# Block products of a sparse attention layer: one 128-column product for a chunk that both halves of a block list, in place of two 64-column products side by side

## The chip, the cores and the metric

The kernel runs on one core of one Trainium2 chip. The metric is the device time of one execution in microseconds (us). A TensorE instruction multiplies a stationary operand (the weights, loaded by a LDWEIGHTS instruction, up to 128 columns) by a moving operand (here 512 columns wide) and adds into a bank of PSUM. A float32 product of this kernel is two such pairs of LDWEIGHTS and MATMUL in the trace. An operand of 64 columns fills half of the array's columns, and its result lies in 64 of a bank's 128 partitions.

## The reference, cut to what matters

`x` is 4096 x 512, `adj` is 4096 x 4096 with about 1% of its entries above zero (weights from 0.05 to 1 at those places, the diagonal always set, the pattern symmetric).

```
# layer 0
h = relu(layernorm(x));  x = x + relu(normalized(adj) @ h @ W + b)
# layer 1
inp = relu(layernorm(x));  h = inp @ W
e = leaky_relu(h @ a[:F] + (h @ a[F:]).T, 0.2);  mask = adj > 0
att =  softmax(where(mask,  e, -1e12), axis=1)
neg = -softmax(where(mask, -e, -1e12), axis=1)
x = x + elu(concat([att @ inp, neg @ inp], axis=1) @ wtrans)
```

The change is in layer 1, in the two products `att @ inp` and `neg @ inp`.

## The kernel before

Layer 0 (to about 960 us) is a dense product with all of `adj`. While it runs, the kernel also makes, from `adj` and for layer 1, lists of the rows that each group of rows needs.

Layer 1 is sparse. The 4096 output rows are cut into 64 blocks of 64 rows, two blocks a pair (`2n` and `2n + 1`). A block is again two halves of 32 rows. The rows of `inp` that a pair needs, with their scores and their mask bytes, are gathered from a table in DRAM into three tiles of SBUF, in chunks of 128 rows: tile 0 with 8 chunks, tile 1 with 7 (6 gathered and, as the last, the pair's own rows), tile 2 with 7 (`LISTED`, `CHUNKS`, lines 43 and 44). The even block of a pair reads tiles 0 and 1, which are its chunks 0 to 14; the odd block reads tiles 1 and 2, its chunks 0 to 13, of which 0 to 6 are tile 1. Tile 1 is so shared by both blocks.

Not every chunk holds rows for both halves of a block. `HALVES` (line 49) lists for the even and the odd block which chunks each half reads:

```python
HALVES = (
    ((0, 1, 2, 3, 4, 10, 11, 12, 13, 14), (3, 4, 5, 6, 7, 8, 9, 10, 11, 14)),
    ((0, 1, 2, 3, 4, 6, 9, 10, 11, 12, 13), tuple(range(11))),
)
```

`weights(r)` (line 1754) makes the attention weights `p` of a block for all its chunks with ScalarE and VectorE: 128 gathered rows by, for each half `h` and each sign `g` of the score, 32 output rows. In `p[:, k]` the four groups of 32 columns lie side by side, so a half is 64 columns (its 32 rows for both signs) and a chunk 128. VectorE then sums `p` over its chunks (line 1787).

`product(r)` (line 1799) is one block's work on TensorE: the sums of the weights (`inverse_sums`, cs, L580), and `half_products` (line 551), the function that is changed. It goes through the two halves' lists side by side: step by step one chunk of half 0 and one chunk of half 1, each a product with 64 weight columns and the 512 columns of the gathered rows, the first into partitions 0 to 63 of the bank `u`, the second into 64 to 127. An even block has 10 such steps, an odd one 11, so a pair has 42 products. In the trace they are `u<-g,p` at L556. ScalarE then scales `u` by the inverse sums into `us` (L1815), TensorE transposes it (tp, L595), and `project1` and `finish1` multiply by `wtrans` (o, L1826). Two more chunks come last for the early pair and the first pair of the loop, from the tile `late_h`, where both halves read both chunks (lines 1574 and 1812).

The order of the loop is written out (line 1903). For block `k` of the order: `product(order[k])`; then gathers for the pair after next (after an even block tile 0, after an odd one tiles 1 and 2); then `weights(order[k + 2])`; then the transposes of block `k - 1`; then half of the projection of an earlier pair. The gathers are indirect DMAs issued by POOL (GpSimd), one for each chunk (L506), and kept in program order. The own rows come through a DMA that SP issues (L520), after the six gathers of tile 1. The tiles are doubled over pairs (`k % 2` in `gather1`, line 1739), and are taken again as whole tiles (`reuse_waits="tile"`): the gathers for the pair after next into a tile wait until the last product that reads the tile has ended. Two early blocks (`product0`, L1567, tile name `p_pair`) are multiplied at the end of layer 0, in the order of the program where `pin` is set. The block products of the loop are not pinned.

Of the kernel before, what the change touches and what calls it, by code (L numbers as in the profile page):

```python
# [32 lines left out]
RB = 64  # L33
# [10 lines left out]
CHUNKS = (8, 7, 7)  # L44
# [4 lines left out]
# [4 lines that stand above are left out]
# [221 lines left out]
def gcn_gat_kernel(  # L274
# [26 lines left out]
    nc = tc.nc  # L301
# [36 lines left out]
    with sbuf(name="init", bufs=1) as init:  # L338
        column = init.tile([P, P], F32, name="column")
        nc.vector.memset(column[:, 0:1], 0.0)  # L340
        n = 1
# [60 lines left out]
    steps = [(c, r) for c in range(NK) for r in range(CAPS[c] // 8)]  # L402
# [148 lines left out]
    def half_products(r, u, p, row, chunks, end=True, pin=False, begin=True):  # L551


        for ks in zip(*chunks):
            for h, k in enumerate(ks):
                i = nc.tensor.matmul(  # L556
                    u[h * RB : (h + 1) * RB],
                    p[:, k, h].rearrange("p g i -> p (g i)"),
                    row(k),
                    start=begin and k == HALVES[r % 2][h][0],  # L560
                    stop=end and k == chunks[h][-1],
                )
                if pin:
                    tc.keep_in_program_order(i)

# [41 lines left out]
    with sbuf(name="y0", bufs=1) as y_pool, sbuf(name="wa", bufs=1) as wa_pool, sbuf(name="bits", bufs=4) as bits_pool, sbuf(name="small0", bufs=4) as small, ExitStack() as rest, ExitStack() as lists:  # L607
# [5 lines left out]
        def list_tables(pool):  # L613
            rank = pool.tile([P, EN], F32, name="rank")
            nc.gpsimd.iota(
                rank,
                [[-1, EN]],
                base=EN,
                channel_multiplier=0,
                allow_small_or_imprecise_dtypes=True,  # L620
            )
            before = pool.tile([P, NE + 1, NH], F32, name="before")
            start = pool.tile([NH, 1], F32, name="start")
            nc.gpsimd.iota(
                start,
                [[0, 1]],
                base=0,
                channel_multiplier=STR,
                allow_small_or_imprecise_dtypes=True,
            )  # L630
            return rank, before, start

        rank, before, start = list_tables(list_pool)
# [400 lines left out]
        def new_rows(pool, n):  # L1034
            rows = [pool.tile([P, ROW_W], F32, tag=f"h{k}", name=f"h{k}", bufs=1) for k in range(n)]
            for h in rows:
                nc.gpsimd.memset(h[:, ROW_T + 1 :], 0.0)
            return rows
# [94 lines left out]
        i0, n = GROUPS[0]  # L1133
# [362 lines left out]
        def early_pair(work, at_pool, prod, rows):  # L1496
# [63 lines left out]
            def product0(r):  # L1560
                u0[r] = bank(f"u{r}")

                def row(k):
                    gt, k0, n = parts0(r)[k >= parts0(r)[1][1]]
                    return gt[:, k - k0, :F].bitcast(F32)

                half_products(r, u0[r], ps0[r], row, HALVES[r % 2], False, r == blocks[0])  # L1567

            def late_product0(r):
                def row(k):  # L1570
                    return late_h[:, k - slots0(r), :F]

                late = range(slots0(r), slots0(r) + n_late)
                half_products(r, u0[r], ps0[r], row, (late, late), begin=False)
                sum0(r, late)
# [77 lines left out]
        with sbuf(name="work0", bufs=2) as work, sbuf(name="rows0", bufs=1) as row_pool, sbuf(name="sums", bufs=3) as sum_pool, sbuf(name="at", bufs=6) as at_pool:  # L1653
# [4 lines left out]
            with tc.manual_schedule(engines=order - {engine.PE}):  # L1658
                rows = new_rows(row_pool, 3)
# [31 lines left out]
    def sparse_layer1():  # L1691
        nonlocal verdict
        with ExitStack() as pools:
# [105 lines left out]
            def product(r):  # L1799
                p, total = wgt.pop(r)  # L1800

                rl = None if r in first else inverse_sums(small, r, total)
                u = bank(f"u{r}")

                def row(k):
                    gt, k0, n = parts(r)[k >= parts(r)[1][1]]
                    return gt[:, k - k0, :F].bitcast(F32)

                half_products(r, u, p, row, HALVES[r % 2], r not in with_late)
                if r in with_late:  # L1810
                    ks = range(n_late)
                    half_products(r, u, lates.pop(r), lambda k: late_h[:, k, :F], (ks, ks), begin=False)
                rl = rl or inverse_sums(small, r, total)
                us[r] = work.tile([P, F], F32, tag="us", name=f"us{r}")
                nc.scalar.activation(us[r], u, AF.Copy, scale=rl)  # L1815
# [169 lines left out]
```

## Time and profile before

| | |
|---|---|
| median of 4 runs | 2025.3 us (2012.46 to 2028.84) |
| the profiled execution | 2015.94 us |
| its span, first to last instruction | 2014.1 us |
| mean granted TensorE clock | 0.98 |
| layer 0, to about 960 us | TensorE busy 947.81 of 960.00 us |
| layer 1 loop, 1100 to 1950 us | TensorE busy 773.01, VectorE 452.38, ScalarE 490.74, POOL 538.19 of 850.00 us |
| end, 1950 to 2014 us, no gathers left | TensorE busy 56.22 of 64.00 us |

In the profile PE is TensorE's matmuls, PEld its weight loads, which overlap with the matmuls, DVE is VectorE, ACT ScalarE, POOL GpSimd and SP the queue of SyncE. A group's line has, in order: line of code, engine, operation, names out<-in, the weights' shape (partitions*columns), the tiles' shapes, the count; then busy time in us and the mean ns of one; then the idle time of the engine just before these instructions and what ended most of it. `g` are the gathered tiles, `p` the attention weights. In the view in order of time, a line is: start, duration, engine, line, operation, names, count, and in brackets the idle time before it with what ended it; instructions that overlap or follow one another closely are merged into one line with their count. In the view of waits a line is: who waited, for what, us in total, how often, the longest. "issue" is idle time for which the profile shows no releaser; "remote" is one that it can't place.

### The profile page before, as it was taken

What the parts mean: (1) busy time and instruction counts of PE and PEld (TensorE: products, weight loads), DVE (VectorE), ACT (ScalarE), POOL (GpSimd) and SP (SyncE); (2) the same over time, 40 slices, a digit from 0 to 9 for tenths busy, and PEclk for the clock granted to TensorE, in tenths of its full rate; (3) what the DMA queues carried; (4) which work ended last, traced back from release to release, by engine and by line L of the source; (5) the groups of instructions that cost most, each with busy time, mean ns of one, the idle gap of its engine ahead of it and who ended that gap; (6) DMA issues with size and microseconds to landing.
All of it is one profiled execution on the core that took longest, in us unless ns stands there. A gap on an engine that the chain in (4) does not pass through costs nothing.

```text
span 2014.1 us, 24509 instructions
## 1 busy us (share of the span) xinstructions
PE 1890.3 (94%) x7708; PEld 1052.6 (52%) x7708; DVE 1272.7 (63%) x2758; ACT 937.3 (47%) x2165; POOL 822.3 (41%) x919
## 2 busy tenths in 40 slices
PE   8999999999999999999679989999899898898988
PEld 3444468888888888884333333333333333333333
DVE  6766588898889979762535655545555465454552
ACT  6777743222223222221436655556565565564551
POOL 3110000024322233305536666566666666666640
PEclk9999999999999999999879999899999999999999
DMA  9999967576858586758857878788888787887860
GB/s 370 396 334 335 321 198 245 175 244 211 265 163 274 171 256 194 243 179 303 266 202 249 278 239 301 235 293 260 282 271 292 241 260 243 265 250 241 259 190 23
DMA packets 217218, 504.33 MB, mean 250 GB/s; under 512 B 35059, under 2 KB 69395, under 8 KB 217078
## 3 DMA queue, kind: packets, MB, share of 16 engines
q0 software_dynamic: 62560, 233.71, 36.3%
q1 hardware_dynamic: 114240, 236.49, 35.1%
q10 hardware_dynamic: 40278, 32.47, 5.2%
q8 instruction: 63, 1.03, 0.2%
q14 instruction: 77, 0.63, 0.1%
HBM read 457.77 MB, written 103.45 MB: 279 GB/s over the span
## 4 chain that ended last, share of the span: by engine, by line
PE 89%; issue 6%; DMA 2%; POOL 2%; DVE 1%; another core or an unknown queue 0%; ACT 0%; ACTq 0%; POOLq 0%; DVEq 0%; SPq 0%
PE p L1105 31%; PE u L556 30%; PE o L1826 10%; PE acc L1064 5%; PE yp L890 5%; PE q L1465 3%; PE tp L595 2%; DMA ar<-in_adj 2%; POOL g L506 2%; PE counts L867 1%; PE cs L1541 1%; PE tx L831 1%; PE o L1860 0%; PE cs L580 0%; DVE key L429 0%
## 5 line engine op out<-in xcount | busy, mean ns | idle before, releaser
L506 POOL DMA_INDIRECT g<-table,idx x672 | 639.5, 952 | 436.0 <-issue 176.4
L556 PE MATMUL u<-g,p 128*64 128x512 f32 x2604 | 622.5, 603 | 87.3 <-issue 75.7
L556 PEld LDWEIGHTS u<-g,p 128*64 128x64 f32 x2604 | 189.3, 138 | 462.6 <-issue 440.1
L442 POOL DMA_INDIRECT ld<-lst,off x160 | 143.7, 898 | 343.2 <-DMA ld<-lst,off 152.1
L1765 ACT ACTIVATE z<-s,g 128x64 f32<-128x64 f32 x812 | 259.6, 320 | 47.1 <-issue 13.3
L1105 PE MATMUL p<-y,at 128*128 128x256 f32 x832 | 248.0, 380 | 0.0
L1105 PE MATMUL p<-y,sums 128*128 128x256 f32 x832 | 247.4, 379 | 0.0
L1105 PE MATMUL p<-t,sums 128*128 128x256 f32 x832 | 245.3, 379 | 0.0
L1826 PE MATMUL o<-wt,ut 128*128 128x512 f32 x496 | 227.0, 601 | 2.1 <-DVE eo L1843 1.4
L1768 DVE TENSOR_TENSOR z<-z,y 128x512 f32<-128x512 f32 (+1 forms) x124 | 80.3, 647 | 204.8 <-ACT y L1767 116.2
L1787 DVE TENSOR_REDUCE total<-p 128x128 f32<-128x1920 f32 (+1 forms) x62 | 207.7, 3350 | 2.1
L1105 PEld LDWEIGHTS p<-t,sums 128*128 128x128 f32 x832 | 158.0, 190 | 21.7 <-issue 0.2
L1105 PEld LDWEIGHTS p<-y,sums 128*128 128x128 f32 x832 | 158.0, 190 | 21.5
L1105 PEld LDWEIGHTS p<-y,at 128*128 128x128 f32 x832 | 157.1, 190 | 23.2 <-issue 2.3
L1826 PEld LDWEIGHTS o<-wt,ut 128*128 128x128 f32 x496 | 91.6, 195 | 94.2 <-issue 92.6
L852 ACT ACTIVATE junk<-ar 128x1024 bf16<-128x1024 f32 x128 | 134.5, 1051 | 9.1 <-DMA ar<-in_adj 4.9
L930 ACT ACTIVATE m<-at 128x1024 uint8<-128x1024 f32 x110 | 113.0, 1047 | 53.1 <-DVE t_all L1032 16.1
L1777 DVE SCALAR_TENSOR_TENSOR p<-g,z 128x512 f32<-128x512 uint8 (+1 forms) x124 | 78.4, 632 | 92.8 <-ACT z L1773 87.1
L1773 ACT ACTIVATE e<-z 128x512 f32<-128x512 f32 (+1 forms) x124 | 67.1, 542 | 149.1 <-issue 66.9
L1777 DVE SCALAR_TENSOR_TENSOR p<-g,e 128x512 f32<-128x512 uint8 (+1 forms) x124 | 79.0, 637 | 85.6 <-DMA g<-table,idx 26.6
L1105 PE MATMUL p<-t,at 128*128 128x256 f32 x416 | 123.9, 380 | 1.2 <-DVE w L975 1.2
L1064 PE MATMUL acc<-y,at 128*128 128x512 f32 x256 | 120.2, 594 | 0.0
(220 smaller groups left out, 2030.1 us busy)
## 6 DMA issues: line engine op xcount, KB each, us to landing
ar<-in_adj SPq DMA_DIRECT2D x128, 512.0 KB
at<-in_adj_t SPq DMA_DIRECT2D x112, 512.0 KB
table<-table SPq DMA_DIRECT2D x49, 1032.0 KB
table<-m ACTq DMA_DIRECT2D x48, 256.0 KB
g<-table,idx POOLq DMA_INDIRECT x672
g<-table SPq DMA_DIRECT2D x32, 322.0 KB
at<-in_adj_t SPq DMA_DIRECT2D x32, 256.0 KB
xr<-in_x SPq DMA_DIRECT2D x32, 256.0 KB
```

The costliest lines, as they stand in the source:

```text
L442: return nc.gpsimd.indirect_dma_start(out=lst_dram[g][e % TURNS][:, :], out_offset=bass.IndirectOffsetOnAxis(ap=off[g][:, e, c : c + 1], a ...
L506: i = nc.gpsimd.indirect_dma_start(out=gt[:, k, :], out_offset=None, in_=table[2 * n // RPT], in_offset=bass.IndirectOffsetOnAxis(ap=idx[n ...
L556: i = nc.tensor.matmul(u[h * RB : (h + 1) * RB], p[:, k, h].rearrange("p g i -> p (g i)"), row(k), start=begin and k == HALVES[r % 2][h][0 ...
L852: nc.scalar.activation(junk, ar, AF.Identity, accum_out=parts[j][:, c : c + 1])
L890: nc.tensor.matmul(yp, hx_t[j][:, c * P : (c + 1) * P], w0_sb[:, c, :], start=c == 0, stop=c == FC - 1,)
L930: nc.scalar.activation(m, at, AF.Sign)
L1064: nc.tensor.matmul(a, at[:, 0, it * P : (it + 1) * P], y0[j], start=j == 0, stop=j == NJ - 1)
L1105: i = nc.tensor.matmul(out, left[:, x * P : (x + 1) * P], right, start=jp == 0 and first, stop=jp == NP - 1 and (final or not first),)
L1765: nc.scalar.activation(z[:, c], s, AF.Identity, bias=t[:, c])
L1777: nc.vector.scalar_tensor_tensor(p[:, k : k + n, :, g], mask.rearrange(four, h=2), 0.0, x.rearrange(four, h=2), ALU.is_gt, ALU.mult,)
L1787: nc.vector.tensor_reduce(total, q, AX.X, ALU.add)
L1826: i = nc.tensor.matmul(halves[j], uts[j][:, g, c, :], wts[g][:, c, :], start=g == 0 and c == 0, stop=g == 1 and c == FC - 1,)
```

## The change

In `half_products` the chunks that both halves list are taken out of the two lists. Each becomes one product with the chunk's 128 weight columns into all 128 partitions of `u`. What is left of the two lists is paired as before. The steps are then sorted, and Python's sort keeps the order of equals: first the steps that read only the block's first tile, then those that read its second tile too.

```diff
-        for ks in zip(*chunks):
-            for h, k in enumerate(ks):
-                i = nc.tensor.matmul(
-                    u[h * RB : (h + 1) * RB],
-                    p[:, k, h].rearrange("p g i -> p (g i)"),
-                    row(k),
-                    start=begin and k == HALVES[r % 2][h][0],
-                    stop=end and k == chunks[h][-1],
-                )
+        both = [k for k in chunks[0] if k in chunks[1]]
+        alone = zip(*[[k for k in ks if k not in both] for ks in chunks])
+        steps = [(k, k) for k in both] + list(alone)
+        steps.sort(key=lambda ks: max(ks) >= CHUNKS[r % 2])
+        for n, (k0, k1) in enumerate(steps):
+            start, stop = begin and n == 0, end and n + 1 == len(steps)
+            if k0 == k1:
+                halves = [(u, p[:, k0].rearrange("p h g i -> p (h g i)"), k0)]
+            else:
+                halves = [
+                    (u[h * RB : (h + 1) * RB], p[:, k, h].rearrange("p g i -> p (g i)"), k)
+                    for h, k in enumerate((k0, k1))
+                ]
+            for rows, left, k in halves:
+                i = nc.tensor.matmul(rows, left, row(k), start=start, stop=stop)
                 if pin:
                     tc.keep_in_program_order(i)
```

The steps of a block, a single number for a chunk of both halves, and (half 0, half 1) for a pair:

| block | before | after |
|---|---|---|
| even | (0,3) (1,4) (2,5) (3,6) (4,7) (10,8) (11,9) (12,10) (13,11) (14,14) | 3, 4, (0,5) (1,6) (2,7), 10, 11, 14, (12,8) (13,9) |
| odd | (0,0) (1,1) (2,2) (3,3) (4,4) (6,5) (9,6) (10,7) (11,8) (12,9) (13,10) | 0, 1, 2, 3, 4, 6, 9, 10, (11,5) (12,7) (13,8) |

## The prediction

> **What bounds the kernel now.** I read the page first, then the waits by engine inside layer 1, then one pair of blocks in order of time. The page says that TensorE is busy 94% of the span, and that the line to be changed, L556, is its largest group.
>
> ```profile
> span 2014.1 us, 24509 instructions
> PE 1890.3 (94%) x7708; PEld 1052.6 (52%) x7708; DVE 1272.7 (63%) x2758; ACT 937.3 (47%) x2165; POOL 822.3 (41%) x919
> L556 PE MATMUL u<-g,p 128*64 128x512 f32 x2604 | 622.5, 603 | 87.3 <-issue 75.7
> L1826 PE MATMUL o<-wt,ut 128*128 128x512 f32 x496 | 227.0, 601 | 2.1 <-DVE eo L1843 1.4
> ```
>
> Two things are to be seen. One product is two MATMUL instructions (2604 = 31 pairs of blocks x 42 chunk products x 2). And 2604 of 603 ns make 1570 us, yet the group is busy 622.5: the 64-column products do run side by side. But nearly all idle time of TensorE in layer 1 stands before this same line, and no releaser is named. So I asked who waits on TensorE and on POOL from 1100 to 1980 us:
>
> ```profile
> PE u L556 <- issue: 75.5, 63, 2.3
> POOL g L506 <- remote: 78.4, 26, 3.2
> POOL g L506 <- PE u L556: 67.5, 26, 5.2
> ```
>
> POOL, which issues the row gathers, stops twice in every pair: 26 times for about 3.0 us with no releaser in sight, and 26 times for a block product. One pair in order of time, POOL first, then TensorE:
>
> ```profile
> 1507.62 0.95 POOL L506 DMA_INDIRECT g<-table,idx  x1 [0.30 <-issue]
> 1508.87 0.95 POOL L506 DMA_INDIRECT g<-table,idx  x1 [0.30 <-issue]
> 1512.79 0.94 POOL L506 DMA_INDIRECT g<-table,idx  x1 [2.98 <-remote]
> ...
> 1521.89 0.94 POOL L506 DMA_INDIRECT g<-table,idx  x1 [0.30 <-issue]
> 1524.77 0.94 POOL L506 DMA_INDIRECT g<-table,idx  x1 [1.93 <-PE u L556]
> ```
>
> ```profile
> 1500.46 7.94 PE L556 MATMUL u<-g,p 128*64 128x512 f32 x34
> 1509.57 0.59 PE L556 MATMUL u<-g,p 128*64 128x512 f32 x1 [1.16 <-issue]
> 1511.66 1.81 PE L556 MATMUL u<-g,p 128*64 128x512 f32 x5 [1.51 <-issue]
> 1513.40 0.66 PE L595 MATMUL tp<-ident,us 128*128 128x128 f32 x4
> 1513.90 3.60 PE L1826 MATMUL o<-wt,ut 128*128 128x512 f32 x8
> 1517.33 0.28 PE L580 MATMUL cs<-ones,total 128*128 128x1 f32 x2
> 1517.54 9.66 PE L556 MATMUL u<-g,p 128*64 128x512 f32 x44
> ```
>
> The even block's 40 instructions stop after 34 and crawl until 1512.4; POOL starts again at 1512.79; the odd block's 44 run without a gap. The next view shows that the stall comes with the gathers: the last pair, when no gather is left, has none (40 in 8.80 us).
>
> ```profile
> 1968.62 8.80 PE L556 MATMUL u<-g,p 128*64 128x512 f32 x40
> 1977.36 0.66 PE L595 MATMUL tp<-ident,us 128*128 128x128 f32 x4
> 1981.49 9.66 PE L556 MATMUL u<-g,p 128*64 128x512 f32 x44
> ```
>
> So a pair is paced by a ring, not by TensorE alone. TensorE's own work in a pair is 8.80 + 9.66 + two times 4.1 (tp, o, cs) = 26.7 us; the pair takes 30.9 (1500.46 to 1531.34). The ring: POOL resumes (1512.79), issues 8 gathers at 1.25 us, waits until the odd block has read the shared tile (1524.77), issues 13 more (16.2 us), and 3.0 us later all goes on (1543.69). The 3.0 us are the same whether TensorE was stopped early or late, so I put them to the gathers, not to TensorE.
>
> **The change part by part.** The profiled execution took 2015.94 us (span 2014.1), 0.46% under the median of 2025.3; differences are worked out in the former and added to the latter.
>
> *Products.* Even blocks had 10 steps of two halves; they get 5 full-width steps and 5 pairs. Odd blocks had 11; they get 8 and 3. The number of steps stays. A pair of instructions side by side takes (9.66 - 0.64)/21 = 0.430 us in the odd block; a full-width one takes (3.60 - 0.60)/7 = 0.429 in o L1826. Over 13 steps x 2 instructions x 31 pairs = 806 slots the gain is at most 0.7 us: zero, and the bounds are -0.7 and +0.7.
>
> *Weight loads.* Two of 138 ns become one of 190 to 195 ns (rows of L556 and L1826). In o L1826 the load lies under the stream (slot 0.43). That is the cover; without it, 806 x 0.05 = 40 us, but the o rows show the full-width load covered, so nothing.
>
> *Changes of width.* From a 64-column to a 128-column product the next start comes 0.53 us after the last (1968.62 + 8.80 - 0.59 to 1977.36) instead of 0.43, and the first one runs 0.05 longer: 0.15 per change. An odd block has as many as before; an even block (full, pair, full, pair) has two more: 0.30 a pair, 31 x 0.30 = 9.3 us if on the path. In 28 pairs the even block ends in the stall, which hides it; taken: 0.3 for the last pair, bounds 0 and 9.3. [...]
>
> *Release of the shared tile.* Tile 1 holds chunks 0 to 6 of the odd block. Before, its last chunk was read in step 7 of 11 (9 beside 6). Now the sort moves 5 into a pair with 11, step 9 of 11, behind a change of width. The release comes 2 x 0.86 + 0.15 = 1.87 us later. Who waits: POOL's 1.93 us wait above, with the 13 gathers queued behind it, and SP's load of the own rows into the same tile. There is slack, though: the trace's semaphore events show POOL let go 0.2 to 0.7 us after that step's end (0.74 in this pair), when the first 8 gathers have drained. Taken: 0.45. Tile 0 is still released by step 5 of the even block, tile 2 at the end of the odd one, as before.
>
> *End of the even block.* Its tile-0 release is at instruction 20 of 40; TensorE got 14 more through before it starved. Behind the release the changed block has 6 full and 8 half instructions, 14 in all, for the same 4.3 us. If what runs out is a supply counted in instructions, the block just finishes in the shadow of the stall, and after the stall TensorE starts with tp: saved is 1512.4 to 1513.40, 1.0 us (0.8 to 1.2). If it runs out after a time (14 half instructions are 3.0 us), about the same work is left as now: saved 0. I take 1.0: across the pairs the starvation keeps to instruction 33 to 38, while the gathers' end moves over several us. [...]
>
> *Sum.* Per pair +1.87 - 1.0 - 0.45 = +0.42 us; there are 28 such pairs (26 in the window and two before it): +11.8, and 0.3 for the last pair: +12. That is 2028 against the profiled execution, 2037 against the median.
>
> The vector work is unchanged. The scaling of u on ScalarE waits for the even block (97.2 us in all) and can only come earlier. Layer 0 isn't touched.
>
> **The rivals.**
> *Late release in full (slower).* Nothing is saved at the even block's end, and the ring grows by 1.87 less the slack: 1.42 x 28 = 40 us, 2065; with the smallest slack 1.67 x 28 = 47, 2072. It decides as soon as less than 0.7 us a pair is saved (0.42 + 0.3 is the 1% of 20 us over 28 pairs). For it: the two waits on the product that are certain in the trace. Against it: the count of 14.
> *The stall goes with the instructions (faster).* Fewer TensorE instructions (60 in place of 80 with the loads) end the crawl. In proportion 75.5 x 20/80 = 19 us, 2006; all of it, 1950. For it: the idle time is called issue, and only half-width products have it. Against it: 3.0 us of POOL idle that don't depend on where TensorE stood, and 44 instructions without a gap.
> *Nothing moves.* Slack and the earlier finish swallow the late release, and the widths cost 0 to 9 us: 2025 to 2034. For it: POOL is often let go only when its own gathers have drained.
> A colder clock could add to either of the slower ones: a starved TensorE is throttled in some pairs already (granted clock 0.98 from 1100 to 1950 us).
>
> **How the numbers follow.** Forecast 0.40, late release 0.32, stall shrinks 0.18, nothing moves 0.10. The likeliest has its own range: -0.07 to +0.87 a pair (saved 0.8 to 1.2, slack 0.2 to 0.74), 2023 to 2050. One per cent, 20 us, is about what a measurement can tell from no change. Faster by more: 0.15, the third case but for its small end. Slower by more: 0.36, the second case and 0.04 of the forecast's upper end. Within: 0.49. The range leaves out 0.10 below (a stall more than half gone) and 0.08 above (late release with more throttling): 1985 to 2075.
>
> **What would show it.** Steps: L556 in two forms, full-width slots of 0.43 us. Release: POOL's second stop longer than 1.93 us, and PE u named. Even end: 30 instructions without a gap and tp before POOL resumes. If POOL's 3.0 us are gone, the third case holds; if the even block crawls at its last pairs as now, the second. The forecast is wrong if the framework orders the unpinned products otherwise than the loop does.

## The result, and the profile after

| | before | after |
|---|---|---|
| median | 2020.47 us (59 runs, 2004.14 to 2032.12) | 2034.83 us (38 runs, 2012.34 to 2053.40) |
| the profiled execution | 2015.94 us | 2041.79 us |
| its span, granted clock | 2014.1 us, 0.98 | 2040.0 us, 0.96 |

The ratio after to before is 1.0049, 95% interval 1.0032 to 1.0066: about 10 us more, within the 1% that was called no change. The two medians lie 14.4 us apart, since that of after holds six slow runs, over 1.5% above its fastest, which the ratio leaves out. The profiled execution of after lies 7.0 us above its median and that of before 4.5 us below, so the two traces differ by 25.9 us, and only the smaller difference is the change's. The traces are good for where things happen; the sizes below come from ratios of times.

First the page after, the lines that answer to those shown of before, with the changed product taken apart by its shapes (two lines of the view of groups by form):

```profile
PE 1907.6 (94%) x6860; PEld 1076.8 (53%) x6860; DVE 1272.5 (62%) x2758; ACT 936.7 (46%) x2165; POOL 827.1 (41%) x919
...
L568 PE MATMUL u<-g,p 128*128 128x512 f32 (+1 forms) x1798 | 643.0, 623 | 77.0 <-issue 76.1
```

```profile
L568 PE MATMUL u<-g,p 128*128 128x512 f32 x806 | 417.2, 650 | 76.3 <-issue 75.8
L568 PE MATMUL u<-g,p 128*64 128x512 f32 x992 | 234.4, 602 | 0.6 <-issue 0.3
```

The product's matmuls fell from 2604 to 1798, its loads as well, and TensorE is no less busy (1907.6 for 1890.3 us). Its idle time without a releaser before the product is what it was: 76.1 for 75.7 us. But it has moved to the full-width form (75.8 of 76.1). Next the waits inside layer 1, from 1100 to 1980 us:

```profile
PE u L568 <- issue: 76.1, 71, 2.9
POOL g L506 <- PE u L568: 54.9, 21, 10.3
POOL g L506 <- remote: 44.5, 19, 3.0
POOL g L506 <- DVE total L1793: 27.9, 3, 9.4
```

TensorE's stall has not changed in sum (75.5 before). POOL's stops have: they were two a pair, the longest 5.2 us; now some are of 9 to 10 us (longest 10.3, and three of some 9 us put down to a VectorE line that had long been done). The view in order of time shows what lies behind. TensorE first, one pair without a stall, and the next pair but one:

```profile
1507.09 9.33 PE L568 MATMUL u<-g,p 128*128 128x512 f32 x30
...
1520.42 9.84 PE L568 MATMUL u<-g,p 128*128 128x512 f32 x28
...
1562.19 9.33 PE L568 MATMUL u<-g,p 128*128 128x512 f32 x30
...
1575.51 1.96 PE L568 MATMUL u<-g,p 128*128 128x512 f32 x4
1578.06 0.59 PE L568 MATMUL u<-g,p 128*128 128x512 f32 x1 [0.59 <-issue]
1580.16 1.00 PE L568 MATMUL u<-g,p 128*128 128x512 f32 x1 [1.51 <-issue]
1583.66 1.01 PE L568 MATMUL u<-g,p 128*128 128x512 f32 x1 [2.50 <-issue]
...
1587.86 9.32 PE L568 MATMUL u<-g,p 128*128 128x512 f32 x20 [1.08 <-issue]
```

The even block now runs its 30 instructions in 9.33 us without a gap, in every pair, and the odd block of a lucky pair its 28 in 9.84. But in every second or third pair the odd block crawls after its first instructions. POOL over the same stretch:

```profile
1559.49 0.94 POOL L506 DMA_INDIRECT g<-table,idx  x1 [2.05 <-PE tp L601]
...
1584.51 0.94 POOL L506 DMA_INDIRECT g<-table,idx  x1 [0.30 <-issue]
1595.75 0.95 POOL L506 DMA_INDIRECT g<-table,idx  x1 [10.29 <-PE u L568]
```

From 1559.49 to 1585.45 POOL issued 21 gathers without a stop (before, the longest run was 13), and TensorE crawled from 1578.06 to 1587.86. Then POOL waited 10.29 us for tile 1, which that same crawling block had still to read. The granted clock from 1100 to 1950 us is 0.93 in this trace, where it was 0.98.

What holds TensorE can be read in the trace's semaphore events, and in who waits for them. Before, the two products of the even block that read tile 0 last had ended at 1504.98. TensorE's next updates on record come at 1512.49 and 1512.53, and POOL, whose 13th gather had ended at 1509.82, issued the next at 1512.79; the last packet of the 13 gathers ended at 1512.76. After, the even block that began at 1562.19 had ended at 1571.52. ScalarE's next instruction scales its result and waits for TensorE alone. It started at 1589.42, 0.8 us after the last packet of the 21 gathers (1588.58):

```profile
1589.42 0.69 ACT L1821 ACTIVATE us<-u,rl 128x512 f32<-128x512 f32 x1 [15.69 <-remote]
```

So TensorE's updates are held back while POOL issues a run of gathers, and in both cases they came out within about 1 us of the gathers' end; TensorE goes on for a while without them (here 5.95 us past 1571.52) and then crawls. Not every update is held to the end: in before, ScalarE read the odd block's result of 1496.40 at 1497.18, while POOL was issuing. Nor is every update on record (from 1100 to 1800 us of before 174, for 249 instructions of TensorE that end in one), so how late they come is better read from the engines that wait for them. In that window VectorE stood idle for over 1 us after the end of cs in 14 of 45 blocks of before (up to 4.9 us), and ScalarE after the end of a block's products in 10 of 44 of after (up to 16.1 us).

### The profile page after: what moved, and what is told of

Same layout as the page of the kernel before. It is cut to its first block, busy times and chain, and to the rows that moved or that the text cites. A ratio compares the mean times of both kernels' runs of the same rounds, so it can differ in the third digit from the quotient of the medians.

```text
span 2040.0 us, 22814 instructions
## 1 busy us (share of the span) xinstructions
PE 1907.6 (94%) x6860; PEld 1076.8 (53%) x6860; DVE 1272.5 (62%) x2758; ACT 936.7 (46%) x2165; POOL 827.1 (41%) x919
## 4 chain that ended last, share of the span: by engine, by line
PE 84%; issue 7%; POOL 2%; DVE 2%; ACT 1%; another core or an unknown queue 1%; DMA 1%; POOLq 0%; ACTq 0%; DVEq 0%
PE p L1111 30%; PE u L568 27%; PE o L1832 9%; PE acc L1070 5%; PE yp L896 5%; PE q L1471 3%; POOL g L506 2%; PE tp L601 1%; DMA g<-table,idx 1%; PE counts L873 1%; PE tx L837 1%; PE cs L1547 1%; ACT z L1771 0%; PE o L1866 0%
## 5 line engine op out<-in xcount | busy, mean ns | idle before, releaser
L568 PE MATMUL u<-g,p 128*128 128x512 f32 (+1 forms) x1798 | 643.0, 623 | 77.0 <-issue 76.1
L568 PEld LDWEIGHTS u<-g,p 128*128 128x128 f32 (+1 forms) x1798 | 219.5, 166 | 450.1 <-issue 441.7
L1821 ACT ACTIVATE us<-u,rl 128x512 f32<-128x512 f32 x62 | 42.7, 688 | 176.1 <-remote 153.6
```

Source lines behind the costliest of these rows:

```text
L568: i = nc.tensor.matmul(rows, left, row(k), start=start, stop=stop)
```

## The experiments

Three theories were put against each other. A, the forecast's: TensorE and POOL form a ring, in which the late release of tile 1 costs and the shorter even block saves. B: only the changes of width cost, on TensorE. C: the gathers' transfers set the mean pace, and what TensorE is spared in one place it loses in another.

**First group: one part at a time.** All four ran on one chip, where the kernel before takes 2003.79 us. The traces of before and after shown above were taken where it takes 2020 us, so the times of one trace are set beside those of the other with care.

*Early release alone.* The changed kernel, with one line more after the sort:

```python
if r % 2 and (11, 5) in steps:
    steps.insert(0, steps.pop(steps.index((11, 5))))
```

> The changed kernel, with the pair of half-width products that reads chunk 5 (11 beside 5) put first in the odd block, so that tile 1 is let go after step 7 or 8 as before, and not after step 9. One more change of width in an odd block. Theory A (the late release of tile 1 is paid on the ring, as forecast): the 1.4 us a pair come back, 28 x -1.0 = -28 us against before, ratio 0.986. Theory B (the changes of width are paid on TensorE, and nothing else): 0.15 us a pair more than the changed kernel, ratio 1.005 to 1.008. Theory C (the gathers' transfers set the mean pace, and what TensorE is spared in one place it loses in another): ratio 1.000 to 1.006, the same as the changed kernel's 1.005, with the stall in another place.

Measured: 0.9913 (0.9881 to 0.9945), 17 us less than before. The waits of its layer 1, from 1100 to 1980 us:

```profile
POOL g L506 <- PE u L570: 75.6, 26, 7.9
PE u L570 <- issue: 31.6, 33, 1.8
POOL g L506 <- remote: 21.6, 10, 3.3
```

TensorE's stall fell from 76.1 to 31.6 us, and POOL's stops without a releaser from 19 to 10. With tile 1 let go after step 7 the rest of the change gains; so the step in which chunk 5 is read is worth about 1.4% of the time (1.0049 / 0.9913 = 1.0137; the two ratios come from different groups of runs). Theories B and C both miss it; A has the sign, at some 60% of its size.

*Order alone.* The changed kernel with full width taken out:

```diff
-            if k0 == k1:
+            if False:
```

> The order of the steps of the changed kernel, but each chunk that both halves list multiplied as two products of 64 columns: no full-width product, no change of width inside the blocks, 84 instructions in a pair as before. Theory A: the release is late by 1.7 us and nothing is saved at the even block's end, 1.25 us x 28 = 35 us, ratio 1.017. Theory B: as before, ratio 1.000. Theory C: ratio 1.000 to 1.003.

Measured: 1.0129 (1.0098 to 1.0160), 26 us more. TensorE does what it did before, instruction for instruction, only in another order. The stall changes its place (same window):

```profile
PE tp L601 <- issue: 44.8, 36, 2.5
PE o L1832 <- issue: 27.4, 27, 2.2
```

44.8 + 27.4 = 72.2 us for 75.5, but no longer before the products: POOL's run of 13 gathers starts later against TensorE, and the crawl begins after the even block's end, at its transposes (tp). The place of a stall says little about its cause.

*Full width in odd blocks only* (and the order that goes with it):

```diff
-        both = [k for k in chunks[0] if k in chunks[1]]
+        both = [k for k in chunks[0] if k in chunks[1] and r % 2 == 1]
...
-            if k0 == k1:
+            if k0 == k1 and r % 2 == 1:
```

> The change in odd blocks only; even blocks multiply and order as before. Theory A: late release in full, 1.4 us x 28 = 40 us, ratio 1.020. Theory B: the odd block's own 0.21 us x 31 = 6.5 us, ratio 1.003. Theory C: ratio 1.000 to 1.003, with the even block's stall as before.

Measured: 1.0093 (1.0063 to 1.0122). The late release is there and no gain: theory A's sign, half its size.

*Full width in even blocks only:* the same with `r % 2 == 0`.

> The change in even blocks only; odd blocks multiply and order as before. Theory A: the release is as before and the even block ends 1.0 us sooner, 28 us in all, ratio 0.986. Theory B: the even block's own 0.56 us x 31 = 17 us, ratio 1.009. Theory C: ratio 1.000 to 1.005, with the even block free of stalls and the stall in the odd block, as in the changed kernel.

Measured: 0.9935 (0.9910 to 0.9959). The even block, with fewer instructions, is through before TensorE starves; what is left of the stall is in the odd block or between the blocks:

```profile
1511.83 0.59 PE L1832 MATMUL o<-wt,ut 128*128 128x512 f32 x1
1513.66 3.16 PE L1832 MATMUL o<-wt,ut 128*128 128x512 f32 x7 [1.23 <-issue]
...
1516.80 9.33 PE L568 MATMUL u<-g,p 128*128 128x512 f32 x30
```

The four roughly add up. Order alone +1.29% and the full-width products with the early release -0.87% make +0.42%; odd blocks +0.93% and even blocks -0.65% make +0.28%; the whole change, in its own runs, is +0.49%. It is two effects, each about two to three times as large as their sum.

**Second group: without the gathers, and fewer changes of width.** These ran on another chip, and there the kernel before takes 1858.88 us (26 runs, 1855.30 to 1865.76), 7 to 8% less than in all runs above.

*The kernel before without gathers:* from the seventh pair on the tiles of the pair two earlier are read again.

```diff
                 k = pairs.index(n)
+                if k >= 6:
+                    gath.setdefault(n, {})[a] = gath[pairs[k - 2]][a]
+                    return
```

> The kernel before, without the gathers (and own-row loads) of layer 1's pairs from the seventh on: these pairs multiply the tiles of the pair two earlier again. It leaves out 24 pairs' 21 gathers; TensorE's work is untouched. Theory A and theory C alike: nothing crawls, a pair takes TensorE's own 26.7 us and not 31.3, so 24 x 4.6 = 110 us less, ratio 0.945. If the crawl were TensorE's own (its instructions, the half-width products), it would stay, ratio 1.00.

*The changed kernel without gathers:* the same lines in it.

> The changed kernel with the same gathers left out. What differs from the kernel before without these gathers is the products alone. Forecast's term (changes of width 0.30 us a pair, products and loads nothing): 7 us more in 24 pairs. Theory B (0.56 us in the even block and 0.21 in the odd one): 0.77 x 24 = 18 us more. Against before: 0.949 or 0.954.

Measured: 1852.25 and 1869.78 us (0.9963, 0.9950 to 0.9976, and 1.0052, 1.0036 to 1.0069). Both expectations were made for the slower sort of chip; here there is no crawl to take away, with the gathers or without. What the pair shows is the products alone: 17.5 us more for the change. One pair of before and one of after, in order of time:

```profile
1525.30 9.66 PE L556 MATMUL u<-g,p 128*64 128x512 f32 x44
...
1539.03 8.80 PE L556 MATMUL u<-g,p 128*64 128x512 f32 x40
```

```profile
1522.92 9.33 PE L568 MATMUL u<-g,p 128*128 128x512 f32 x30
...
1536.25 9.84 PE L568 MATMUL u<-g,p 128*128 128x512 f32 x28
```

The median pair takes 26.60 and 27.17 us: the change costs TensorE 0.57 us a pair (31 x 0.57 = 17.7), with fewer instructions. Within these blocks a full-width start follows the last after 0.43 us, and so does a pair side by side; the loads (137 and 160 ns in the mean) hide in both, with 0.0 us of TensorE's idle time before the products. All that is added is at the changes. Against the plain 0.43 the distances of the starts add 0.14 us from full to half width and 0.20 back; behind cs 0.12 for a half-width start and 0.08 for a full-width one; and 0.15 from half width to tp. Before, that is 2 x 0.12 + 2 x 0.15 = 0.54 a pair; after, 0.08 + 0.14 + 0.20 + 0.14 + 0.15 in the even block and 0.08 + 0.14 + 0.15 in the odd one, 1.08.

*Two changes of width in every block* (the even one of the change has four, counted with its border to tp). Full-width steps of the first tile, then all pairs, then the other full-width steps, so that tile 1 is let go after step 7, as before the change:

```diff
-        steps = [(k, k) for k in both] + list(alone)
-        steps.sort(key=lambda ks: max(ks) >= CHUNKS[r % 2])
+        late = [k for k in both if k >= CHUNKS[r % 2]]
+        steps = [(k, k) for k in both if k not in late] + list(alone) + [(k, k) for k in late]
```

> The changed kernel with the steps in another order, in both blocks: the full-width steps of the tile that is let go first, then all pairs of half-width products, then the other full-width steps. Tile 0 is let go after step 5 and tile 1 after step 7, as before the change; a block begins and ends in full width, so that each has two changes of width and not four. Theory A with the release worth about 1 us a pair (changed kernel 1.005 against 0.991 with the early release): 0.991 or less; the changes of width spared, 0.3 to 0.5 us a pair, bring it to 0.983 to 0.987. Theory C: 0.991, since what TensorE is spared is lost again in the wait for the gathers.

Measured: 1.0039 (1.0024 to 1.0053) on this chip, pairs of 26.91 us: 0.25 less than the change, still 0.31 more than before (by the distances above 2 x (0.08 + 0.14 + 0.20) = 0.84, which is 0.30 over 0.54). This trace also shows the ring on a chip without holds. POOL's stops are short or absent: up to 147 gathers follow one another without a stop over 1.2 us, and no update of TensorE is over 0.1 us late (mean 0.01 us). The gathers are issued as fast as elsewhere, 1.25 us apart. Here TensorE is the bound (busy 714.68 of the 720.00 us from 1100 to 1820), and the change costs what its instructions cost.

**Third group: what holds the updates.** On the first chip again (before: 1998.28 us).

*Control.* The kernel before, with gathers into the same tile objects, so that each waits for its own chunk:

```diff
-                gt = g_pools[k % 2, a].tile(...)
+                if k < 6:
+                    gt = g_pools[k % 2, a].tile(...)
+                else:
+                    gt = gath[pairs[k - 2]][a]
```

> The kernel before, but from the seventh pair on the gathers go into the same tile objects as two pairs earlier, so that a gather waits for the reads of the chunk that it overwrites and not for the whole tile. All rows are gathered. Theory A (the ring of release and POOL's issue sets the pace): releases come earlier by up to 1.9 us for tile 1, so up to 24 x 1.9 = 46 us less, ratio 0.977 to 1.00. Theory C (the transfers set the pace): ratio 1.00. It is also the control of the next kernel.

Measured: 0.9998 (0.9975 to 1.0021). Letting go chunk by chunk gains nothing here, the far end of what theory A allowed: POOL's stops are as many (2.2 a pair) and shorter (2.2 us for 2.8 in the trace of before, in the mean), and TensorE's updates are held as before: VectorE stood idle for over 1 us after cs in 15 of 46 blocks.

*Half the bytes.* The same, and from the seventh pair on `out=gt[:, k, :ROW // 2]` from a table seen as rows of 322 words.

> The same, with gathers of half the bytes: from the seventh pair on a gather brings 322 of 644 words of a row, as many gathers and as many rows. What it leaves out is the other half of each row; the output is not the reference's. Theory C (transfers): the pair falls to TensorE's 26.7 us and the crawl goes, 24 x 4.6 = 110 us less than the control, ratio about 0.945. Theory A (POOL's issue of 21 x 1.25 = 26 us and its waits): as the control, within 1%.

Measured: 0.9988 (0.9967 to 1.0010). The queue of the gathers from 1200 to 1800 us (packets, MB, and the share of the 16 DMA engines' time that they took), control first, then half:

```profile
q0 software_dynamic: 32722, 134.90, 69.5%
```

```profile
q0 software_dynamic: 19744, 67.87, 41.1%
```

Half the bytes and 28 points less of the DMA engines' time change nothing that the times can tell. Theory C, in the form that the transfers' throughput sets the pace, falls.

**Last group: three on a third chip,** where before takes 2019.52 us.

*Two changes of width once more,* on a chip that holds.

> The kernel with two changes of width in a block, once more, for a chip on which TensorE's updates are held while POOL issues gathers (there the kernel before takes some 2000 us; where they are not held it takes 1859 us and TensorE's own time sets the pair). On a holding chip: releases as before and fewer instructions in the even block, as in the run with the early pair (0.991) and the run with full width in even blocks only (0.9935): 0.985 to 0.993. On the other kind: 1.004 as measured.

Measured: 0.9872 (0.9840 to 0.9905), 26 us less than before. What is left of TensorE's stall, from 1100 to 1800 us:

```profile
PE u L568 <- issue: 22.3, 24, 1.5
PE o L1832 <- issue: 19.5, 16, 3.2
```

On this chip it is faster than the kernel before (the whole change was not run here), and on the chip of the second group it is not (1.0039).

*Spaced gathers.*

```diff
                 tc.keep_in_program_order(i)
+            if gap is not None:
+                tc.keep_in_program_order(nc.gpsimd.memset(gap, 0.0))
```

> The kernel before, with a small POOL memset (128x64, some 0.15 us) after each gather from the seventh pair on, so that gathers are issued every 1.4 to 1.5 us and not every 1.25. POOL's issue of a pair becomes 30 us. Theory rate (updates are held because gathers come too fast for something): the holds and POOL's two stops go, a pair takes about 30 us, ratio 0.985 to 0.995 on a holding chip. Theory drain (an update waits until POOL's gathers have ended, whatever their spacing): the stops of 2 to 3 us stay, 30 + 4.8 = 35 us a pair, ratio 1.035 to 1.045. On a chip that doesn't hold: 30 us against 26.9, ratio about 1.04.

Measured: 0.9993 (0.9970 to 1.0017). The edit did not do what it was made for:

```profile
1441.24 0.17 POOL L517 MEMSET gap<- 128x64 f32 x1
1441.57 0.95 POOL L506 DMA_INDIRECT g<-table,idx  x1 [0.16 <-issue]
```

The memset went into the 0.30 us that POOL spends between two gathers; they start every 1.28 us for 1.25. Whether slower gathers would end the holds was so not tested.

*Without the gathers, on a chip that holds.*

> The kernel before without the gathers of layer 1's pairs from the seventh on, once more, for a holding chip. If the crawl comes with the gathers: a pair of 26.6 us as on the other chip, (31.3 - 26.6) x 24 = 113 us less, ratio 0.944. If the chip itself slows TensorE in layer 1: more than that, up to 1.00.

Measured: 0.9431 (0.9391 to 0.9470), pairs of 26.60 us from the seventh on, the same as on the other chip to the hundredth. What was left of the stall, from 1100 to 1800 us, came in the pairs that still gathered:

```profile
PE u L556 <- issue: 3.4, 5, 1.2
```

The crawl comes with the gathers; the chip doesn't slow TensorE by itself.

Over the last 24 pairs with gathers, POOL's stops over 1.2 us, counted in the view in order of time, tell how a pair is paced on the holding chips: 21 x 1.25 = 26.3 us of issue, and the stops (less the 0.3 us that stand between any two gathers).

| kernel | before takes there, us | stops a pair | mean us | over 5 us, of all 24 pairs | pair us |
|---|---|---|---|---|---|
| before | 2020 | 2.00 | 2.79 | 1 | 31.31 |
| after | 2020 | 1.75 | 3.68 | 8 | 32.37 |
| order alone | 2004 | 2.00 | 2.98 | 0 | 31.73 |
| odd blocks only | 2004 | 2.00 | 2.98 | 1 | 31.73 |
| early release alone | 2004 | 1.58 | 2.87 | 1 | 30.49 |
| even blocks only | 2004 | 1.96 | 2.55 | 1 | 30.65 |
| two changes, third chip | 2020 | 1.79 | 2.89 | 1 | 30.89 |
| two changes (no holds) | 1859 | 0.29 | 2.11 | 1 | 27.28 |

For before: 26.3 + 2.00 x (2.79 - 0.30) = 31.3. Pairs compare only within one chip. On the first chip the stop before the gathers into tile 1 shows what the late release costs: 2.25 us in the mean with the release as before (even blocks only), 3.15 and 3.18 with the late one (order alone, odd blocks only), 0.9 us a pair more. In the whole change this stop is mostly short (median 2.2 us), but 8 of the 24 are of 6.9 to 10.3 us; such long ones do not come with the late release alone. With the early release some stops go (1.58 a pair). That the fewer instructions let TensorE post its releases in time is argued and not shown: with full width in even blocks alone the stops are as many (1.96) and only shorter (2.55 us).

## Why the prediction was right, step by step

The total came out as forecast, +10 us for +12 (the 2037 us started from 2025.3, the median of the first four runs of before). Its two large terms had the right sign and cause, but both were some 1.5 to 2 times too large. They have opposite signs, so the errors nearly cancelled: that the total is so close is luck.

- *Products: right.* Slots of 0.43 us in both forms; nothing gained.
- *Weight loads: right.* 204 ns for the full-width load (view by form), under the stream; no slot got longer.
- *Changes of width: the cause right, the size wrong.* 0.57 us a pair was measured on the chip without holds, 0.30 was predicted, and 17.5 us in all lie outside the bounds of 0 to 9.3. The step counted the changes, two more, at 0.15 each. It missed that a change inside a block costs 0.14 to half width and 0.20 back, while behind the small cs product a half-width start is hardly dearer (0.12) than a full-width one (0.08): the border that goes saves less than a change inside adds. How much of the 17.5 us the stall hides on the other chips was not measured by itself.
- *Release of the shared tile: right, and smaller.* 1.87 less 0.45, 1.42 us a pair and 40 us were predicted; order alone measured 26 us, 0.92 a pair, and the stop before tile 1's gathers grew by 0.9. The slack was not read rightly: in 10 of the last 24 pairs the trace of before lets POOL go within 0.15 us of the step's end, and in the mean 0.33 us after it, not 0.2 to 0.7. Nor is it a fixed slack: when TensorE's updates are held, the release is posted only when POOL's own gathers have drained, and in the whole change that costs 9 us at once now and then.
- *End of the even block: right, and smaller.* Predicted -1.0 us a pair, -28; the full-width products with the early release measured -17 (what their changes of width cost included), full width in even blocks alone -13. That what runs out is counted in instructions and not in time was assumed and is not shown. From the start of POOL's run of 13 to the crawl TensorE got 57 to 61 matmuls and 13.7 to 15.0 us in before, and 46 to 57 matmuls and 13.8 to 17.1 us with full width in even blocks. These ranges don't decide between a count and a time. The block got through with room to spare: that its stall would vanish altogether, and come back in the odd block, was not foreseen.
- *What would show it.* Two forms and 0.43 us: seen. The even block's 30 without a gap: seen. POOL's second stop longer than 1.93 us with PE u named: seen where POOL had stopped first; elsewhere it is gone, or 9 to 10 us.
- *POOL's 3.0 us "put to the gathers, not to TensorE": right.* After a run of 13 gathers POOL stops for 2.7 to 3.1 us in nearly every pair of before, order alone and even blocks only, whatever the products are. But what it waits for is TensorE: the update of tile 0's last product, which is held until about the gathers' end (1512.53 above). This step was missing in the ring.
- *The rivals.* "Late release in full" (+40 to +47 us) names the cause that takes the gain away, but not in full. "The stall goes with the instructions" was half true: the stall was 31.6 us, for 75.5 in the trace of before, once the release was put back. "Nothing moves" fits the total and not one of its parts. The colder clock was there (0.93), and goes with the long crawls: 0.78 from 1565 to 1596 us, where the crawl above lies, and 1.00 in the 31 us ahead of it.

Open: why TensorE's updates are held while POOL issues gathers, and why one of the three chips of the experiments does not do it. Half the bytes changed nothing (0.9988); the gathers' rate was not tested.

## What to carry to other kernels

When a change of the work also moves the step that lets a shared buffer go, try the two apart: here each was worth about two or three times their sum, and putting one product back to the front of its block turned a loss of 0.5% into a gain of 0.9%. Keep products of one width together, and let a block begin and end in the width of its neighbours: here that took back 0.25 of 0.57 us a pair. A stall with no releaser that wanders when the order changes, as with order alone, need not belong to the line that it stands before; here it belonged to a ring of releases.

## What the runs showed of the hardware that was not expected

- The same kernel took 1858.88 us on one chip and 1998 to 2020 us on the others; with no gathers from the seventh pair on, a pair takes 26.60 us on the one and on one of the others. Layer 0 is as busy on each (TensorE 947 to 951 of 960.00 us); the difference lies behind it, and goes with how late TensorE's semaphore updates come while POOL issues gathers: never over 0.1 us on the one; on the others engines stood idle for them for up to 16.1 us.
- While its updates are held, TensorE starts a matmul every 1.4 to 3.5 us, as in 1578.06, 1580.16 and 1583.66 above (2.10 and 3.50 apart, for the plain 0.43), and runs on at about the time when the gathers have drained (1587.86, and the last packet at 1588.58).
- Half the bytes of every gather: no change (0.9988).
- A change from 64 to 128 weight columns cost 0.20 us and back 0.14, beside slots of 0.43.
- A memset of 0.17 us between two gathers cost POOL 0.03 us: they start every 1.28 us for 1.25.
